# A two-layer graph kernel on one core: weight scaling moved into round 1, a new order of copies from shared PSUM tiles, ACT tables loaded by dummies, decodes issued four blocks ahead

## The chip, the cores and the metric

The kernel runs on one core of one Trainium2 chip. The metric is the device time of one execution in microseconds (us), given as the median of the fast runs; all runs of this study were in the fast state. A ratio is the mean time of one kernel's fast runs over the mean of the other kernel's fast runs of the same rounds, so it is not quite the ratio of the medians quoted beside it. Intervals are 95% intervals.

The engines are called PE (the matmul engine; PEld is its weight load), DVE (VectorE), ACT (ScalarE), POOL (GpSimd) and SP (the queue that issues most transfers).

## The reference, cut to what matters

The reference has N = 3327 nodes with D = 64 features and a dense adjacency of N x N.

```python
# layer 0: attention in hyperbolic space
h = maximum(layernorm(x), 0)
x_t = logmap0(h, c)
left, right = x_t @ w_att[:D, 0], x_t @ w_att[D:, 0]
adj_att = sigmoid(left[:, None] + right[None, :] + b_att) * adj
x_local = logmap(h[:, None, :], h[None, :, :], c)            # N x N x D, never formed by the kernel
x = x + proj(expmap(h, einsum('ij,ijd->id', adj_att, x_local), c), c)
# layer 1: the last <= 100 neighbours of a row, weighted by powers of one half
h = maximum(layernorm(x), 0)
support = h @ weight
mask = adj != 0
rank = cumsum(mask, axis=1);  deg = rank[:, -1:];  k = minimum(deg, 100.0)
pos = rank - (deg - k)
w = mask * where(pos > 0, 0.5 ** (k - pos), 0.0)
x = x + w @ support + bias
```

## The kernel before

The adjacency is worked on in four strips of node columns (8, 8, 6 and 4 blocks of 128). Each strip runs over the 26 row blocks in rounds. In a round, PE forms the pair products `pq`, counts neighbours into `pc` and sums into `po`; ACT takes two Gelu passes over `pq` and makes the sigmoids `sg`; DVE makes the mask and two products, and DVE or ACT reads the counts out as bytes (`behind_lo`, `behind_hi`). Three parts matter here.

**The start.** The node features are turned by PE and copied out of PSUM into `ju` (by DVE) and `jz` (by ACT). A Newton chain and two logarithms then give the factors of the attention logits.

```python
    rsqrt(V, pre, y, v, NB)                       # layer norm
    ...
    def kept(pt, bs, at):
        n = bs.stop - bs.start
        V.tensor_copy(ju[: KB + 7, bs], pt[: KB + 7, at : at + n, :])
        A.copy(jz[:, bs], pt[:, at + n : at + 2 * n, :])
    ...
    p1 = ps.tile([P, 16, P], F16, name="pq", bufs=2)
    turned_to(p1, first_i, 0)                     # PE transposes nu and nz into ONE tile
    p2 = ps.tile([P, 4, P], F16, name="po")
    turned_to(p2, last_j, 0)
    kept(p1, first_i, 0)
    strip_in(0)
    kept(p2, last_j, 0)
    V.tensor_scalar(x2c, x2, MIN_NORM, None, op0=ALU.max)
    rsqrt(V, pre, yr, x2c, NB)                    # three Newton steps, after the copies
    ...
    A.activation(g, g2, AF.Ln, bias=one_c, scale=-0.5)
    ...
    def last_of_ahead():                          # a generator, advanced in rounds 0 and 1
        ...
        yield
        logits((later,))
        left_to_dram()
        yield
        V.tensor_mul(hw[:, :13, :D], rl[:, :13], wide(wn[:, :13], 13))
```

**The change of strip.** At the end of a strip PE transposes its sums into one PSUM tile (`turn`), and two copies bring them to SBUF.

```python
    def per_node(k, pa):
        ...
        for c in range(0, nb, 4):
            ...
            if c == 0:
                A.copy(to, of)
            else:
                V.tensor_copy(to, of)
        return post(agg, k)
```

**The last stage.** ACT and DVE decode 22 of the 26 blocks from bytes in turns to bf16 bit patterns (`wt`, seven buffers; the other four are kept ready, `weight_of` in the traces), and PE multiplies each of the 26 with the features `s` of layer 1. The last strip's nodes are finished meanwhile in small portions (`advance`). Then follow the last blocks, a closing product with the scaled weight `w2s`, and the transfer out.

```python
    w2s = const.tile([P, D], F32, name="w2s")
    V.tensor_scalar(w2s, w2, 2.0**27 / HS, None, op0=ALU.mult)
    ...
        for i, j in enumerate(order):
            if j not in weights:
                weights[j] = decode(j)
            asked_of_act()
            advance(LAST)                         # LAST = 6
            for n in range(len(chunks)):
                add(j, weights[j], n)
            ...
        finish()
        for j in range(late, NB):
            weights[j] = decode(j)
        ...
        for n in range(len(chunks)):
            for j in range(late, NB):
                add(j, weights[j], n)
            ...                                   # copy pw[n] out, then close(n - 2) with w2s
```

## Time and profile before

| Kernel before | us |
|---|---|
| median of the fast runs | 437.38 (437.25 to 437.47, 3 runs) |
| span of the profiled run | 434.5 |
| DVE's first product of adjacency and sigmoid (end of the start) | 42.28 |
| PE's first block of the last stage | 374.57 |
| last closing matmul | 426.83 |

The first view is the page of the kernel before. The first line gives each engine's busy time, its share of the span and its instructions; the row PEclk gives PE's granted clock in tenths in 40 slices of the span.

```profile
PE 364.4 (84%) x1460; PEld 155.8 (36%) x1460; DVE 377.1 (87%) x556; ACT 365.0 (84%) x409; POOL 111.4 (26%) x218
PEclk9999699999999899999999899999996999999987
```

The dips in PEclk (slices 5, 14, 23, 31 and the last two) are worth a look: PE loses clock in the start, at each change of strip and at the end. The trace has no clock record before 40.4 us; PEclk shows full clock there, but PE's 512-column matmuls took 0.63 us at 35.9 us and 0.38 us at 41.3 us. The next view is PE's timeline of the kernel before at the first change of strip (start, duration, engine, line, operation, number of matmuls; in brackets the idle time before and who ended it).

```profile
146.09 1.09 PE L1088 MATMUL po<-ident,sg 65*128 65x65 f32 x8 [1.86 <-ACT sg L1082]
146.97 0.63 PE L629 MATMUL pc<-mask,ca 128*128 128x512 bf16 x1
150.00 3.59 PE L668 MATMUL po<-sg,hw 128*65 128x512 f32 x8
```

PE sits idle for 1.86 us ahead of the transposes, and the matmuls after it take 0.63 us each instead of 0.38: half rate, by the clock records (0.50 from 146.2 to 149.6). So this idle time seems to cost more than itself; the runs below test it. The last view is the table of windows of the kernel before at the third change of strip (stretch, length, busy time and count of PE, PEld, DVE, ACT and POOL, then PE's clock, the transfers' share, GB/s). Its stretches are the steps of 3.41 us at whose edges the trace's clock records change.

```profile
323.68:327.09 3.41, 0.42 (x7) 0.30 (x6) 1.49 (x4) 3.09 (x5) 0.00 (x0) 1.00 0.00 0
327.09:330.50 3.41, 2.21 (x6) 0.83 (x6) 3.38 (x6) 1.01 (x2) 0.86 (x4) 0.50 0.51 154
330.50:333.91 3.41, 3.41 (x6) 0.97 (x5) 2.19 (x3) 2.83 (x4) 2.77 (x8) 0.50 0.20 35
```

After a step in which PE was busy for only 0.42 us, the next runs at clock 0.50. PE is idle for part of that one too (2.21 us busy), and a second at 0.50 follows it, in which PE is full.

### The profile page before, as it was taken

Reading aid. Unit: us, or ns where it says so; the run is one execution under the profiler, and the core shown is the slowest. Engines: PE = TensorE matmul, PEld = TensorE weight load, DVE = VectorE, ACT = ScalarE, POOL = GpSimd, SP = SyncE. Lnnn points to the kernel's source line nnn. Section 1 sums busy time; section 2 is a strip of 40 time slices with the busy share of each in tenths; the row PEclk is TensorE's granted clock in tenths of the full one; section 3 lists DMA queues with packets and bytes.
Section 4 is the critical chain, followed back from the end, with each engine's and each line's share of the span. In section 5 each row is a group of like instructions: output and inputs, shape, how many; then the busy total and the mean of one; then the engine's idle time right before and its main releaser. Section 6 shows DMA issues by size and latency. Waiting matters only on the chain.

```text
span 434.5 us, 4704 instructions
## 1 busy us (share of the span) xinstructions
PE 364.4 (84%) x1460; PEld 155.8 (36%) x1460; DVE 377.1 (87%) x556; ACT 365.0 (84%) x409; POOL 111.4 (26%) x218
## 2 busy tenths in 40 slices
PE   0227499999999899999999899999777999877983
PEld 0014233333333333333333454444332333333453
DVE  2776999999999899999999898899988899688931
ACT  3429599999999989999999899999894999399720
POOL 6010000000000035780160083921505183404200
PEclk9999699999999899999999899999996999999987
DMA  8310444545447435543446354444633320000012
GB/s 186 140 38 0 137 147 144 154 151 172 147 150 206 126 122 159 178 148 99 143 121 181 85 148 141 145 129 138 185 106 99 103 90 0 2 0 1 2 25 62
DMA packets 23248, 48.98 MB, mean 113 GB/s; under 512 B 8713, under 2 KB 9169, under 8 KB 23215
## 3 DMA queue, kind: packets, MB, share of 16 engines
q1 hardware_dynamic: 21087, 47.81, 36.6%
q10 hardware_dynamic: 1808, 0.46, 0.6%
q0 software_dynamic: 320, 0.33, 0.5%
q8 instruction: 13, 0.21, 0.2%
q14 instruction: 20, 0.16, 0.1%
HBM read 46.40 MB, written 0.87 MB: 109 GB/s over the span
## 4 chain that ended last, share of the span: by engine, by line
DVE 38%; ACT 23%; PE 22%; issue 10%; POOL 3%; DMA 2%; POOLq 0%; DVEq 0%; ACTq 0%
DVE sg L1173 11%; DVE sg L1154 10%; PE po L668 8%; ACT sg L651 6%; ACT pq L1147 5%; DVE behind_lo L644 3%; ACT pq L1148 3%; PE pc L629 2%; PE pq L658 2%; PE pq L659 2%; PE pc L630 2%; DVE wt L1207 2%; ACT wt L1205 2%; DVE behind_hi L644 2%; ACT behind_lo L640 2%
## 5 line engine op out<-in xcount | busy, mean ns | idle before, releaser
L668 PE MATMUL po<-sg,hw 128*65 128x512 f32 (+1 forms) x364 | 161.1, 566 | 0.4 <-DVE st L895 0.4
L1173 DVE SCALAR_TENSOR_TENSOR sg<-pq,sg 128x1024 f32<-128x1024 f32 (+1 forms) x91 | 103.8, 1140 | 6.6 <-ACT pq L1148 5.3
L1154 DVE SCALAR_TENSOR_TENSOR sg<-sg,ad 128x1024 f32<-128x1024 f32 (+1 forms) x91 | 103.9, 1142 | 2.5 <-ACT sg L651 2.4
L651 ACT ACTIVATE sg<-left_b,right 128x1024 f32<-128x1024 f32 (+2 forms) x103 | 99.5, 978 | 1.0 <-DVE right L819 1.0
L1147 ACT ACTIVATE pq<-pq 128x1024 f32<-128x1024 f32 (+1 forms) x90 | 86.1, 957 | 4.4 <-PE pq L659 4.3
L1148 ACT ACTIVATE pq<-pq 128x1024 f32<-128x1024 f32 (+1 forms) x90 | 85.2, 946 | 2.9
L630 PE MATMUL pc<-mask,cb 128*128 128x512 bf16 (+1 forms) x182 | 66.9, 378 | 16.3 <-DVE mask L618 14.8
L629 PE MATMUL pc<-mask,ca 128*128 128x512 bf16 (+1 forms) x175 | 65.6, 375 | 13.6 <-DVE behind_hi L644 5.8
L668 PEld LDWEIGHTS po<-sg,hw 128*65 128x65 f32 x364 | 49.5, 138 | 70.1 <-issue 55.1
L658 PE MATMUL pq<-iu,ju 71*128 71x512 f16 (+1 forms) x182 | 68.6, 377 | 1.1 <-ACT jz L755 0.4
L659 PE MATMUL pq<-iz,jz 128*128 128x512 f16 (+1 forms) x182 | 67.0, 375 | 0.0
L618 DVE TENSOR_SCALAR mask<-ad 128x1024 bf16<-128x1024 f32 (+1 forms) x91 | 59.0, 649 | 0.0
L630 PEld LDWEIGHTS <-cb 128*128 128x128 bf16 x182 | 18.1, 99 | 69.7 <-issue 52.0
L1218 PE MATMUL pw<-wt,s 128*128 128x512 bf16 (+1 forms) x154 | 33.9, 371 | 7.4 <-DVE wt L1207 5.1
L967 POOL TENSOR_TENSOR dots<-dots,ih 128x8 f32<-128x8 f32 (+1 forms) x3 | 2.6, 876 | 141.1 <-DVE dots L987 141.1
L629 PEld LDWEIGHTS <-ca 128*128 128x128 bf16 x175 | 17.5, 100 | 30.3 <-issue 18.6
L1218 PEld LDWEIGHTS <-s 128*128 128x128 f16 x182 | 18.0, 100 | 26.8 <-issue 9.3
L658 PEld LDWEIGHTS <-ju 71*128 71x128 f16 x182 | 18.2, 100 | 23.9 <-DVE sg L1173 5.2
L640 ACT ACTIVATE behind_hi<-pc 128x1024 uint8<-128x1024 f32 (+2 forms) x24 | 20.7, 864 | 7.1 <-PE pc L630 7.1
L659 PEld LDWEIGHTS <-jz 128*128 128x128 f16 x182 | 18.4, 101 | 19.9 <-issue 3.5
L640 ACT ACTIVATE behind_lo<-pc 128x1024 uint8<-128x1024 f32 (+2 forms) x29 | 24.9, 858 | 0.0
L1223 POOL TENSOR_TENSOR x_sb<-x_sb,bias_b 128x256 f32<-128x256 f32 (+1 forms) x6 | 9.9, 1660 | 49.6 <-DVE w L1056 44.0
(290 smaller groups left out, 364.8 us busy)
## 6 DMA issues: line engine op xcount, KB each, us to landing
ad<-in_adj_t SPq DMA_DIRECT2D x65, 512.0 KB, 3.6
ad<-in_adj_t SPq DMA_DIRECT2D x26, 384.0 KB, 3.1
out<-o SPq DMA_DIRECT2D x6, 128.0 KB, 2.0
left_b<-left_d SPq DMA_DIRECT2D x1, 512.0 KB, 3.3
x_sb<-in_x ACTq DMA_DIRECT2D x1, 416.0 KB, 5.7
x_sb<-in_x SPq DMA_DIRECT2D x1, 416.0 KB, 4.9
iz<-jz SPq DMA_DIRECT2D x3, 128.0 KB, 2.4
left_b<-left_d SPq DMA_DIRECT2D x1, 384.0 KB
```

The lines of the kernel that those rows point to most:

```text
L618: V.tensor_scalar(*args, 0.0, None, op0=ALU.not_equal)
L629: T.matmul(S.pc[:, f0:f1], ca, S.before[:, f0:f1], start=False, stop=True, skip_group_check=True)
L630: T.matmul(S.pc[:, f0:f1], cb, now[:, f0:f1], start=S.first, stop=True, skip_group_check=True)
L640: A.activation(kept, S.pc[:, : S.F], AF.Relu, scale=128.0 if j in JD else 1.0)
L651: A.activation(part(n, sg, j), S.left[:, : S.F], AF.Tanh, bias=right[:, j : j + 1], scale=0.5)
L658: T.matmul(part(n, pq, j, f0, f1), ju[:KB, j, :], S.iu[:, f0:f1], start=True, stop=False)
L659: T.matmul(part(n, pq, j, f0, f1), jz[:, j, :], S.iz[:, f0:f1], start=False, stop=True)
L668: T.matmul(S.po[: D + 1, f0:f1], hw[:, j, :], part(n, sg_of[n], j, f0, f1), start=j == NB - 1, stop=j == 0)
L1147: A.activation(pq, pq, AF.Gelu, scale=-WG / QS)
L1148: A.activation(pq, pq, AF.Gelu, scale=WH)
L1154: V.scalar_tensor_tensor(sg, sg, 1.0, ad_of.pop(n)[:, :w], op0=ALU.add, op1=ALU.mult)
L1173: V.scalar_tensor_tensor(sg, pq, WD, sg, op0=ALU.add, op1=ALU.mult)
```

## The change

The intent is to take waits off DVE and PE where the engines are not full: in the start, at the changes of strip, and in the last stage. No arithmetic is removed. The core of the diff:

```diff
-PORTIONS, LAST = (2, 4, 4, 8), 6
+PORTIONS, LAST = (2, 4, 4, 8), 8
+LEAD = 4
 ...
     w2 = const.tile([P, D], F32, name="w2")
+    w2s = const.tile([P, D], F32, name="w2s")
 ...                                    # start: two tiles by kind, Newton chain cut in two, tables by dummies
-    p1 = ps.tile([P, 16, P], F16, name="pq", bufs=2)
-    turned_to(p1, first_i, 0)
-    p2 = ps.tile([P, 4, P], F16, name="po")
-    turned_to(p2, last_j, 0)
-    kept(p1, first_i, 0)
+    guess(V, yt, yr, x2c)
+    newton(V, yt, yr, x2c, 1)
+    for src, dst, rows in ((nu, ju, KB + 7), (nz..., jz, P)):
+        pt = ps.tile([P, 16, P], F16, name="pq", bufs=2)
+        ...                             # transposes of src into pt, then copies by DVE (ju) or ACT (jz)
     strip_in(0)
-    kept(p2, last_j, 0)
-    rsqrt(V, pre, yr, x2c, NB)
+    A.activation(load_table, one_c, AF.Ln)
+    newton(V, yt, yr, x2c, 2)
 ...
+    A.activation(load_table, one_c, AF.Gelu)
 ...                                    # last_of_ahead: logits one round earlier
+        logits((later,))
+        left_to_dram()
         wn, opx = small("wn"), small("opx")
 ...
         yield
-        logits((later,))
-        left_to_dram()
-        yield
+        V.tensor_scalar(w2s, w2, 2.0**27 / HS, None, op0=ALU.mult)
 ...
-                    yield LATER if kwargs.get("op") == ALU.pow else 1
+                    yield from [LATER] * 2 if kwargs.get("op") == ALU.pow else [1]
 ...                                    # per_node
             if c == 0:
+                V.tensor_copy(to, of)
+            else:
                 A.copy(to, of)
-            else:
-                V.tensor_copy(to, of)
 ...
-    w2s = const.tile([P, D], F32, name="w2s")
-    V.tensor_scalar(w2s, w2, 2.0**27 / HS, None, op0=ALU.mult)
 ...
+        every = [*order, *range(late, NB)]
 ...
         for i, j in enumerate(order):
-            if j not in weights:
-                weights[j] = decode(j)
+            for jn in every[: i + 1 + LEAD]:
+                if jn not in weights:
+                    weights[jn] = decode(jn)
 ...                                    # the blocks after the loop: decoded there only if not done yet
```

In `kept`, used for later blocks, ACT's copy now also comes ahead of DVE's; `w_h` is computed earlier.

More of the change, by code (lines that the diff above doesn't have):

```diff
@@ L507, in fast, with guess, newton @@
                                 "f_c"))
-    def rsqrt(E, pool, y, v, n):
-        t = pool.tile([P, n], F32, name="rs_t")
+    def guess(E, t, y, v):
         E.tensor_scalar(t.bitcast(I32), v.bitcast(I32), 1, None, op0=ALU.logical_shift_right)
         E.tensor_scalar(y.bitcast(I32), t.bitcast(I32), -1.0, float(0x5F3759DF), op0=ALU.mult, op1=ALU.add)
-        for _ in range(3):
+    def newton(E, t, y, v, steps):
+        for _ in range(steps):
             E.tensor_mul(t, y, y)
@@ L518, in rsqrt @@
             E.scalar_tensor_tensor(y, t, 1.5, y, op0=ALU.add, op1=ALU.mult)
+    def rsqrt(E, pool, y, v, n):
+        t = pool.tile([P, n], F32, name="rs_t")
+        guess(E, t, y, v)
+        newton(E, t, y, v, 3)
     def wide(t, n):
@@ L715, in fast @@
         V.tensor_reduce(rs[:, hs], sr[:, hs], AX.X, ALU.add)
+    w_h = const.tile([P, 2, 2], F16, name="w_h")
+    V.tensor_copy(w_h[:, 0], w_lr)
+    V.tensor_sub(w_h[:, 1], w_lr, w_h[:, 0])
     V.tensor_scalar(v, ss, 1.0 / D, EPS_LN, op0=ALU.mult, op1=ALU.add)
@@ L753, in kept @@
         n = bs.stop - bs.start
+        A.copy(jz[:, bs], pt[:, at + n : at + 2 * n, :])
         V.tensor_copy(ju[: KB + 7, bs], pt[: KB + 7, at : at + n, :])
-        A.copy(jz[:, bs], pt[:, at + n : at + 2 * n, :])
     V.scalar_tensor_tensor(yz, nrm, zs_c, y, op0=ALU.mult, op1=ALU.mult)
@@ L772, in fast @@
     rest(last_j)
-    p1 = ps.tile([P, 16, P], F16, name="pq", bufs=2)
-    turned_to(p1, first_i, 0)
-    p2 = ps.tile([P, 4, P], F16, name="po")
-    turned_to(p2, last_j, 0)
-    kept(p1, first_i, 0)
+    x2c, yr, yt, s, g3 = (small(n) for n in ("x2c", "yr", "yt", "s", "g3"))
+    V.tensor_scalar(x2c, x2, MIN_NORM, None, op0=ALU.max)
+    guess(V, yt, yr, x2c)
+    newton(V, yt, yr, x2c, 1)
+    ends = [*range(first_i.start, first_i.stop), *range(last_j.start, last_j.stop)]
+    for src, dst, rows in ((nu, ju, KB + 7), (nz.rearrange("p b c d -> p b (c d)"), jz, P)):
+        pt = ps.tile([P, 16, P], F16, name="pq", bufs=2)
+        for at, b in enumerate(ends):
+            T.transpose(pt[:rows, at, :], src[:, b, :], id16)
+        for bs, at in ((first_i, 0), (last_j, 8)):
+            copy = A.copy if dst is jz else V.tensor_copy
+            copy(dst[:rows, bs], pt[:rows, at : at + bs.stop - bs.start, :])
     strip_in(0)
-    kept(p2, last_j, 0)
     p3 = ps.tile([P, 16, P], F16, name="pq", bufs=2)
-    x2c, yr, s, g3 = (small(n) for n in ("x2c", "yr", "s", "g3"))
-    V.tensor_scalar(x2c, x2, MIN_NORM, None, op0=ALU.max)
-    rsqrt(V, pre, yr, x2c, NB)
+    load_table = pre.tile([P, 1], F32, name="load_table")
+    A.activation(load_table, one_c, AF.Ln)
+    newton(V, yt, yr, x2c, 2)
     V.tensor_mul(s, x2c, yr)
@@ L797, in fast @@
     A.activation(g3, g3, AF.Square, bias=q0_c, scale=Q1)
+    A.activation(load_table, one_c, AF.Gelu)
     features(later)
     rounded(later)
-    w_h = const.tile([P, 2, 2], F16, name="w_h")
-    V.tensor_copy(w_h[:, 0], w_lr)
-    V.tensor_sub(w_h[:, 1], w_lr, w_h[:, 0])
     V.scalar_tensor_tensor(g3, g3, QK, s, op0=ALU.add, op1=ALU.mult)
@@ L1156, in fast @@
             edges(m + 1)
-        if n == 1:
-            next(rest_of_ahead)
         if two:
@@ L1208, in decode @@
             return wt
-        weights = {j: decode(j) for j in order[: len(JD) + 1]}
+        every = [*order, *range(late, NB)]
+        weights = {j: decode(j) for j in every[: len(JD) + 1]}
         stages.append(Stage(per_node(len(STRIPS) - 1, pa)))
@@ L1237, in fast @@
         for j in range(late, NB):
-            weights[j] = decode(j)
+            if j not in weights:
+                weights[j] = decode(j)
         ow = [l1.tile([P, 512], F32, name="ow", bufs=4)[:, : f1 - f0] for f0, f1 in chunks]
```

## The prediction

> **What bounds the kernel now.** I read the page first: a span of 434.5 us with DVE busy 87%, PE 84% and ACT 84%, so no engine is free and each stage has to be asked by itself. Next I cut the span into stages with a table of windows (first column the stretch, then its length, then busy time and instruction count of PE, PEld, DVE, ACT, POOL).
>
> ```profile
> 0.00:42.00 42.00, 11.88 (x78) 7.34 (x79) 25.38 (x84) 20.49 (x27) 8.49 (x30) 1.00 0.33 94
> 58.00:137.00 79.00, 78.89 (x274) 29.97 (x273) 78.86 (x88) 77.99 (x80) 0.00 (x0) 1.00 0.50 153
> 150.00:234.00 84.00, 82.45 (x281) 30.83 (x280) 82.37 (x89) 81.66 (x87) 35.13 (x62) 1.00 0.46 140
> 373.00:417.00 44.00, 35.83 (x171) 16.52 (x170) 34.34 (x75) 32.02 (x18) 11.60 (x11) 0.99 0.00 1
> ```
>
> In the first two strips PE, DVE and ACT are all full: nothing in the change removes work there, so nothing is to be won inside a strip. The slack is in the start (0 to 42 us), at the three changes of strip, and in the last stage (from 373 us), where the 26 decoded blocks are multiplied. I then read those three in the timelines of single engines (start, duration, engine, line, operation; in brackets how long the engine sat idle first, and who ended it).
>
> ```profile
> 13.01 0.20 DVE L1190 TENSOR_SCALAR w2s<-w 128x64 f32<-128x64 f32 x1 [4.16 <-DMA w<-in_weight]
> 13.12 1.02 DVE L694 SCALAR_TENSOR_TENSOR d<-m,x_sb 128x832 f32<-128x832 f32 x1
> 28.39 0.69 DVE L754 COPY ju<-pq 78x1024 f16<-78x1024 f16 x1 [1.92 <-PE pq L750]
> 42.28 1.23 DVE L1154 SCALAR_TENSOR_TENSOR sg<-sg,ad 128x1024 f32<-128x1024 f32 x1 [2.09 <-ACT sg L651]
> 148.31 0.43 DVE L1100 COPY agg<-po 128x260 f32<-128x260 f32 x1 [1.76 <-ACT agg L1098]
> 325.61 0.29 DVE L1100 COPY agg<-po 128x130 f32<-128x130 f32 x1 [1.92 <-ACT agg L1098]
> ```
> ```profile
> 32.58 1.28 ACT L794 ACT_TABLE_LOAD   x1 [2.17 <-DVE g L792]
> 405.81 8.70 ACT L1205 ACTIVATE wt<-behind_hi 128x3328 uint16<-128x3328 uint8 x3
> ```
> ```profile
> 328.29 0.59 PE L629 MATMUL pc<-mask,ca 128*128 128x512 bf16 x1 [4.19 <-DVE behind_hi L644]
> 414.57 3.22 PE L1218 MATMUL pw<-wt,s 128*128 128x512 bf16 x10 [2.27 <-ACT wt L1205]
> ```
>
> The scaling w2s stands at the end of the source, but the scheduler put it fourth in DVE's queue, where it waits 4.16 us for the last of seven small GpSimd-issued loads, and the second half of the layer norm waits behind it. At the strip changes DVE sits still until ACT, busy with two Gelu passes, has copied its half of the transposed sums. At the end PE's last phase waits for ACT's last three decodes, which ACT could not start before 405.8.
>
> [...] two copies out of one tile run one after the other (the waits of 1.76 and 1.92 us above). So their order is a real choice. [...] a 128x4 pow on POOL took 1.41 us with DVE quiet and 2.62 and 2.59 us when a DVE decode (1.89 us) ran. [...] after the first strip change 512-column matmuls start 0.43 us apart instead of 0.22.
>
> **The change, part by part**, with the order of instructions in both programs (DVE gains three rows, ACT two; PE and POOL keep their counts).
>
> 1. w2s out of the start. The second d (L694) can start at about 8.75 instead of 13.12, which is 4.3 us. Not all of it survives: the next in the queue are masks of the first two adjacency blocks, and the trace's completion signals put those loads at 8.5 and 12.1 us. So the second mask runs from 12.2 and its successor at 12.8, against 15.26: **2.5 us**, less 0.3 for w_h, moved up to before v (its load lands at 12.6, long before). Left: 2.2 us at v.
>
> 2. Transposes in two tiles by kind, half of a Newton chain in front of the copies, tables by dummies. PE transposes from 24.25 (26.46 less 2.2). DVE does six small operations (1.3 us at about 0.22) while it would have waited 1.92 us; ju is copied at 25.55, the rest of the chain ends in g at 28.35 (before: 32.49). ACT copies jz from 26.55 to 27.85, loads Ln's table at once (1.28), takes a dummy (0.2), then Ln and squares (1.12), Gelu's table (1.28), a dummy (0.2), two casts (1.96), and starts Gelu at 34.0 against 38.20. The first sigmoid block waits for PE's transposes of left (36.3 shifted by two casts plus 1.73 and 1.58, so 37.3); DVE's first product starts at about **38.5 against 42.28, 3.8 us**.
>
> 3. Round 0 takes the logits and left_to_dram from round 1. In DVE's queue they now come right after the ju copy, and their matmuls (32 in 1.01 us) need the PSUM tile that this copy frees: DVE waits about 1.1 us, and about 0.3 for the turned left. Before, 0.29 was lost there. The product of round 2, at 54.80 before, comes at about 52.1; the 0.43 us that DVE then waited for PE falls away, since PE and ACT now lead by some 7 us. **Start in all: about 3.0 us.** As DVE is full through the first strip, it hands this on, no more.
>
> 4. Strip changes. DVE copies first, so at 147.2 (end of the PE transposes) instead of 148.31: 1.1 us of DVE, but PE has no gap in the 3 us after and is full after that, so I count 0.3 for the first two changes together. At the third, DVE's copy comes at about 324.2 instead of 325.61, and PE's 4.19 us wait hangs on the DVE work behind it: **1.3 us**.
>
> 5. Last stage. PE needs 26 blocks of 1.39 us, 36 us, and has 44, so its waits decide. I laid DVE's new order out with the old durations: 11 decodes at 1.80 are 19.8 us; what else ran on DVE from 373.53 to its last decode's end at 413.0 is 39.5 less 19.8 less 4.6 idle, 15.1 us; the copy of agg_last adds 0.4. Waits that I expect: 0.55 for transposes, and for POOL 0.2, 0.45, 0.95 and 0.95, in all 3.1. The end is 373.5 + 19.8 + 15.1 + 0.4 + 3.1 = 411.9. ACT now does two decodes instead of three after its last cast and waits: its last ends near 411.0. The last strip's features come later than before (10 decodes ahead of them instead of 8: about 409.9 against 407.6), but still before the last decode. PE's final phase starts at 411.9 instead of 414.57: **2.7 us**. The 20 us after it stay.
>
> Sum: 3.0 + 0.3 + 1.3 + 2.7 = 7.3. 437.4 - 7.3 = **430.1 us**.
>
> **Rivals.** (a) The adjacency loads swallow the start: if the second lands later than 12.1 in an execution, or the logits' wait in round 0 is nearer 2 us, 1.5 us are left of the start: 431.6. For it: 3.4 MB are queued at once; against it: the loads do not depend on the change. (b) The last stage turns on the features: [...] the features land at 412 or later; nothing is won there, 432.8. For it: three waits of 0.9 us on POOL already. Against it: DVE has work in between. (c) DVE's slack at the strip changes does count, because all engines are within 1% of each other, and PE stays at full clock: 2 to 3 us more, 427.5. For it: DVE waited 5.7 us there in sum. Against it: PE has no gap before the features of the third change. (d) The gains are hidden by the full middle: if PE and ACT, not DVE, were what filled strip 1, the start still shifts all of them, so I give this little.
>
> **Range and chances.** (a) and (b) together give 434, (c) with a better end 426.5; the range is 426.5 to 433.5. Faster by over 2% means under 428.6, 1.5 us below my number with an error of some 3 us: 0.30. Slower by 2% would need a new wait of 16 us: 0.01.
>
> **What would show it.** Right: no wait for in_weight on DVE, the second mask near 12.2 with a wait on its load, DVE's first sg product near 38.5, a DVE wait of about 1 us at the logits of round 0, the third strip change's PE wait near 2.9, PE's last phase starting about 7 us earlier than 414.57. Wrong: a first product that is earlier by 3.8 but a first strip that ends no earlier; a PE wait on s instead of wt in the last stage; PE waits that shrink at the first two strip changes.

## The result and the profile after

The changed kernel took **425.63 us** (median of 4 fast runs, 424.87 to 427.22), the kernel before 437.31 us in the same rounds (4 runs, 437.19 to 437.47). The ratio is 0.9737 [0.9709, 0.9766]: faster by more than 2%, and 0.9 us below the range that had been given.

The page of the changed kernel's profiled run (span 423.7 us) has these two lines.

```profile
PE 361.3 (85%) x1437; PEld 155.1 (37%) x1460; DVE 377.9 (89%) x557; ACT 364.6 (86%) x410; POOL 114.0 (27%) x218
PEclk9999989999999999999999899999998999999987
```

The busy times are those of before to within 1% on PE, DVE and ACT: what was removed is idle time. (PE's count is lower because some matmul records are missing from this trace; PEld's is the same.) In PEclk the dip in the start is smaller and one slice later (8 in slice 6 in place of 6 in slice 5), that of slice 31 is smaller (8 in place of 6), and that of slice 14 is gone. DVE's timeline in the changed kernel follows, at the start and at the first and third change of strip.

```profile
8.91 1.03 DVE L702 SCALAR_TENSOR_TENSOR d<-m,x_sb 128x832 f32<-128x832 f32 x1
...
12.06 0.69 DVE L626 TENSOR_SCALAR mask<-ad 128x1024 bf16<-128x1024 f32 x1 [1.52 <-DMA ad<-in_adj_t]
...
38.60 1.23 DVE L1169 SCALAR_TENSOR_TENSOR sg<-sg,ad 128x1024 f32<-128x1024 f32 x1 [1.12 <-ACT sg L659]
...
44.46 0.17 DVE L832 TENSOR_TENSOR left<-po,yr 128x16 f32<-128x16 f32 x1 [1.03 <-PE po L830]
...
144.18 0.43 DVE L1113 COPY agg<-po 128x260 f32<-128x260 f32 x1 [0.28 <-PE po L1103]
...
319.88 0.43 DVE L1113 COPY agg<-po 128x260 f32<-128x260 f32 x1 [0.45 <-PE po L1103]
```

The wait of 4.16 us for the weight is gone; a wait of 1.52 us for the second adjacency block takes part of its place. The first product is 3.68 us earlier than at 42.28. At the changes of strip DVE waits 0.28 and 0.45 us for the transposes, where it had waited 1.76 and 1.92 us for ACT's copy. ACT's timeline in the start of the changed kernel:

```profile
27.82 1.28 ACT L801 ACT_TABLE_LOAD   x1
29.11 0.20 ACT L801 ACTIVATE load_table<-one_c 128x1 f32<-128x1 f32 x1
...
33.63 1.00 ACT L845 ACTIVATE pq<-pq 128x1024 f32<-128x1024 f32 x1
```

The table is loaded at 27.82 (1.28 us; the copy before it ended at 27.80, and ACT's next instruction starts at 29.11) while DVE still works on what the logarithms need, and the first Gelu is at 33.63 instead of 38.20. PE's timeline in the changed kernel, at the first change of strip, at the third, and at the end of the last stage:

```profile
143.44 0.71 PE L1103 MATMUL po<-ident,sg 65*128 65x65 f32 x8 [1.74 <-ACT sg L1097]
...
145.72 3.61 PE L676 MATMUL po<-sg,hw 128*65 128x512 f32 x8
...
322.69 0.38 PE L637 MATMUL pc<-mask,ca 128*128 128x512 bf16 x1 [2.85 <-DVE behind_hi L652]
...
367.89 5.78 PE L1230 MATMUL pw<-weight_of,s 128*128 128x512 bf16 x27
...
402.63 0.60 PE L1230 MATMUL pw<-wt,s 128*128 128x512 bf16 x2 [2.29 <-DVE s L1087]
...
404.43 3.60 PE L1230 MATMUL pw<-wt,s 128*128 128x512 bf16 x9 [0.25 <-DVE wt L1218]
```

Here are the surprises. At the first change PE's idle time is 1.74 us, nearly as before, but PE takes 2.28 us from the transposes to the sums at 145.72, where it had taken 3.91 us (146.09 to 150.00): it did not go to half rate (the clock records have 1.00 from 60.1 to 237.6). At the third change the idle time is 2.85 us instead of 4.19. In the last stage PE's longest wait is now for the features `s`; its final nine matmuls start 36.54 us after its first block (367.89), before 40.00 us.

To compare the sums by part, I use landmarks that both traces have: DVE's product of round 2 (end of the start), the products of rounds 26 and 30 (around the first change), 50 and 62 (second), 76 and 82 (third), and PE's first block of the last stage. The second profile is the same kernel, unedited, in a later run (below).

| Part | predicted gain | changed kernel | same kernel again |
|---|---|---|---|
| start, and the first strip up to round 26 | 3.0 | 2.66 | 2.61 |
| first change (rounds 26 to 30) | 0.3 with the second | 1.60 | -0.02 |
| second change (rounds 50 to 62) | | -0.02 | -0.03 |
| third change (rounds 76 to 82) | 1.3 | 2.41 | 2.43 |
| last stage, from PE's first block to the end | 2.7 | 4.10 | 4.09 |
| **whole span, with the small rest** | **7.3** | **10.79** | **9.12** |

The start is 0.3 to 0.4 us less than predicted; all the surplus lies at the changes of strip and in the last stage.

The figure for the start hangs on which execution it is compared with. Five of the profiled kernels have the start of the kernel before (itself, and the copy order, PE busy, both of these, and the lead, each on it); in them the product of round 26 comes at 139.00, 140.46, 139.94, 139.99 and 139.00 us. In the five profiles with the start of the changed kernel it comes at 136.25 to 136.39. So the table compares with one of the two quickest; against the mean of the five (139.68) the start gains 3.4 us.

### The profile page after: what moved, and what is told of

The parts are those of the page before. It is cut to its first block, busy times and chain, and to the rows that moved or that the text cites. A ratio compares the mean times of both kernels' runs of the same rounds, so it can differ in the third digit from the quotient of the medians.

```text
span 423.7 us, 4689 instructions
## 1 busy us (share of the span) xinstructions
PE 361.3 (85%) x1437; PEld 155.1 (37%) x1460; DVE 377.9 (89%) x557; ACT 364.6 (86%) x410; POOL 114.0 (27%) x218
## 4 chain that ended last, share of the span: by engine, by line
DVE 32%; ACT 28%; PE 21%; issue 12%; POOL 2%; DMA 2%; SPq 0%; POOLq 0%; DVEq 0%; ACTq 0%
ACT sg L659 9%; DVE sg L1186 8%; ACT pq L1162 8%; PE po L676 8%; DVE sg L1169 7%; DVE wt L1218 3%; ACT pq L1163 3%; ACT behind_lo L648 3%; PE pq L666 2%; DMA ad<-in_adj_t 2%; PE pq L667 2%; DVE behind_lo L652 2%; ACT behind_hi L648 2%; PE pc L638 2%; PE pc L637 2%
## 5 line engine op out<-in xcount | busy, mean ns | idle before, releaser
L637 PE MATMUL pc<-mask,ca 128*128 128x512 bf16 (+1 forms) x166 | 60.7, 366 | 15.6 <-DVE behind_hi L652 7.0
L638 PE MATMUL pc<-mask,cb 128*128 128x512 bf16 (+1 forms) x172 | 62.4, 372 | 12.9 <-DVE mask L626 10.6
```

What stands on the lines that cost most here:

```text
L637: T.matmul(S.pc[:, f0:f1], ca, S.before[:, f0:f1], start=False, stop=True, skip_group_check=True)
L638: T.matmul(S.pc[:, f0:f1], cb, now[:, f0:f1], start=S.first, stop=True, skip_group_check=True)
```

## The experiments

The theory that I went in with: the excess is PE's clock. PE falls to half rate for a step of about 3.4 us after a step with little work (in the kernel before at 327.09, after 0.42 us of work in 3.41), and idle time removed at a change of strip or in the last stage removes such steps too. A rival: DVE's time at the changes of strip simply counts in full, and PE's clock follows without costing anything. A second rival for the last stage: the lead of the decodes is worth more than my layout said, whatever the clock does. The twelve kernels ran in three batches, each on another chip, so kernels of different batches are compared only by their ratio to the kernel before (436.44, 436.32 and 435.99 us there). All gave correct outputs.

### The scaling alone

```diff
+    w2s = const.tile([P, D], F32, name="w2s")        # next to w2
 ...
+        V.tensor_scalar(w2s, w2, 2.0**27 / HS, None, op0=ALU.mult)   # last part of last_of_ahead
 ...                                    # its two lines near the end of the source are taken out
```

> Kernel before with w2s moved into round 1 and nothing else. Theory A (the prediction's step 1): DVE's second d starts near 8.9, the second mask waits for its load until 12.1, everything after is 2.5 us earlier, and as all engines move together the time falls by 2.2 to 2.7 us (to about 434.9). Rival B (PE's clock): PE's half-rate windows of 3.4 us fall elsewhere, and one window more or fewer moves the time by a further 1.7 us, so anything from 433 to 436.5, with the span tracking the granted clock.

Measured: 434.37 us (9 runs), ratio 0.9953 [0.9938, 0.9969], 2.07 us by the medians. In the profile the first product came 2.29 us earlier. The step of the prediction that gives 2.2 us at this point holds. What of it reaches the end is less sharp: this profile is 1.68 us ahead at round 26 and 1.30 at round 90, and a further 1.7 us of its span come from the last stage, where this run has no half-rate step. The interval of the ratio is 1.4 to 2.7 us. This is what the expectation's rival B allowed for.

### The copy order alone

```diff
             if c == 0:
-                A.copy(to, of)
+                V.tensor_copy(to, of)
             else:
-                V.tensor_copy(to, of)
+                A.copy(to, of)
```

> Kernel before with DVE copying its half of the transposed sums first at the strip changes, nothing else. Theory S (slack): DVE's waits of 1.76, 2.03 and 1.92 us shrink to about 0.3 to 0.5 us, and about 1.3 us at the first and the third change each reach the end: 2.5 to 3 us. Theory C (clock): PE restarts at half rate after the first change whichever copy is first, so only the third change pays: 1.0 to 1.4 us. The prediction's step 4 said 1.6.

Measured: 433.53 us (6 runs), ratio 0.9939 [0.9919, 0.9960]. The times gain 2.9 us, as theory S said (2.5 to 3), but not where it said: that agreement is luck. The profile's gain at the third change is 2.41 us, at the second -0.10 and at the first -0.05, although DVE did get its copy early there; it loses 1.45 us up to round 26 (the scatter of the start, above) and gains 2.6 us in the last stage, where this run has no half-rate step. DVE's timeline in this kernel at the first change:

```profile
148.28 0.43 DVE L1098 COPY agg<-po 128x260 f32<-128x260 f32 x1 [0.28 <-PE po L1088]
...
156.07 1.22 DVE L644 TENSOR_SCALAR behind_hi<-pc 128x1024 uint8<-128x1024 f32 x1 [2.16 <-PE pc L630]
```

DVE's wait ahead of the copy fell from 1.76 to 0.28 us, and 8 us later DVE stood 2.16 us for PE, whose clock records show half rate from 149.0 to 152.4:

```profile
145.60:149.00 3.40, 1.54 (x14) 0.99 (x14) 3.12 (x6) 3.27 (x5) 0.00 (x0) 1.00 0.53 154
149.00:152.40 3.40, 3.40 (x8) 1.15 (x7) 3.40 (x5) 3.40 (x6) 0.00 (x0) 0.50 0.44 119
```

What DVE had won, it lost to a slower PE. At this change DVE's time seems to count only if PE keeps its clock (here 0.50 in the step from 149.0); the next runs test that.

### PE kept busy at the changes

The product matmuls of the round at the end of a strip are repeated twice into the same PSUM tile, with the same values, so that PE has no gap there.

```diff
         if 0 < n < R - 1:
             products(n + 1)
+            if ended and len(js(n + 1)) == 1:
+                again(n + 1, 2)           # the same matmuls, start=True, into the same pq tile
```

> Kernel before; in the round of each of the first two strip changes PE computes the next product block three times instead of once (same result, written over itself), to fill its gap of 1.86 and 1.94 us before the transposes with work. Theory C (clock): the half-rate windows at 146.2 and 241.8 are gone, PE's next sums start up to 1.7 us earlier, and the time falls by 1 to 3 us. Theory S: DVE is still held until ACT's copy (148.3), so nothing or under 0.5 us.

Measured on the kernel before: 434.81 us (18 runs), ratio 0.9962 [0.9949, 0.9974]. More work made the kernel faster, by 1.6 us by the medians: the profile gains 1.06 us from round 26 to 50 (0.62 of it by round 30), 1.13 at the second change and 0.4 at the third, and the half-rate steps at the first two changes (146.2 and 241.8 in the kernel before) are gone. The transposes of the first change now come with no idle time ahead of them:

```profile
147.02 0.71 PE L1096 MATMUL po<-ident,sg 65*128 65x65 f32 x8
```

> Kernel before with both: DVE copies first, and PE's gap filled. If both are needed at the first change (DVE free at once and PE at full rate), the gain is more than the sum of the two single ones, 4 us or more, with the first change alone giving 1.6 us as in the changed kernel. If the two are independent, the gain is their sum.

Measured with the copy order as well: 431.24 us (5 runs), ratio 0.9879 [0.9860, 0.9899]. The first change gains 1.54 us, the second 1.54 and the third 2.43. From round 26 to 50 the copy order alone gave -0.07, the clock alone 1.06, both 1.54; at the second change they gave -0.10, 1.13 and 1.54: the copy order's 1.5 us of DVE are there to be had, and here they were kept only where PE had no half-rate step. By the times the two parts together (0.0121) are not clearly more than their sum (0.0099); the traces show it, not the times.

### The changed kernel again, unedited

> The changed kernel itself, for its spread on another chip. Theory C (clock): its runs spread over 2 us or more, and the span falls as the granted clock rises, about 1.7 us for each half-rate window of 3.4 us (0.004 of the mean clock). If the spread has another cause, span and clock don't go together. Profile: I expect the windows at the first strip change to be absent or present by chance, as PE's gap there is still 1.7 us.

Measured: 426.84 us (5 runs), ratio 0.9773 [0.9757, 0.9789]. It kept nothing at the first change. The windows of this run around PE's idle time there, cut at the edges of its clock records:

```profile
140.28:143.69 3.41, 1.54 (x10) 0.57 (x8) 3.41 (x5) 3.29 (x5) 0.00 (x0) 1.00 0.47 121
143.69:147.10 3.41, 3.41 (x15) 1.63 (x14) 2.84 (x5) 3.38 (x5) 0.00 (x0) 0.50 0.33 115
```

The first profiled run of the changed kernel around the same idle time, cut in the same way:

```profile
138.64:142.05 3.41, 3.06 (x12) 0.93 (x10) 3.41 (x4) 3.38 (x5) 0.00 (x0) 1.00 0.48 155
142.05:145.46 3.41, 1.97 (x14) 1.23 (x16) 3.13 (x5) 3.38 (x5) 0.00 (x0) 1.00 0.51 154
```

In the first run the idle time was split over two steps, with 3.06 and 1.97 us busy, and the clock stayed at 1.00. In the second it fell wholly into one step, with 1.54 us busy, and the next step was at 0.50. The edges of the steps lie differently against the kernel's start in the two runs: at 138.64 in the first, at 140.28 in the second. So the 1.60 us of the first change in the first profile goes with where the idle time fell on the steps: PE's timeline of the repeated run shows the same program with nearly the same idle time (1.86 us, before 1.74), and half rate after it.

```profile
143.47 1.00 PE L1103 MATMUL po<-ident,sg 65*128 65x65 f32 x8 [1.86 <-ACT sg L1097]
...
147.40 3.59 PE L676 MATMUL po<-sg,hw 128*65 128x512 f32 x8
```

From the transposes to the sums it took 3.93 us here, against 2.28 us in the first profile. Other traces bear this out: of the six with the new copy order and no added work at the changes, the two without a half-rate step at the first change (the changed kernel, and it with the lead taken back) gain 1.60 and 1.62 us there, and the four with one gain between -0.05 and 0.00.

Busy time as these traces count it does not separate the steps that lost full rate from those that kept it. In the kernel before, steps with 1.67 us busy kept it (at 306.6 and 395.4); in the changed kernel one with 1.67 us lost it (at 415.1), and one with 1.70 us kept it (at 39.6). Over the fourteen traces, steps with 1.53 and 1.55 us busy kept it (at 397.3 with PE busy at the changes, at 411.4 with the scaling alone), and in the start 1.91 and 2.17 us lost it (at 41.3 with PE busy everywhere, at 42.9 with the lead taken back).

### PE kept busy in the changed kernel

The same edit as above, on the changed kernel.

> The changed kernel with PE's gaps at the first two strip changes filled by repeating the next product block. Theory C: no half-rate window near 143 and 238; the second change keeps 1.5 us as it did with both edits on the kernel before, so 1.5 to 2 us faster than the changed kernel, and less spread. Rival: the windows there are hidden behind DVE, so no change.

Measured: 423.32 us (5 runs), ratio 0.9717 [0.9694, 0.9741], on the same chip as the repeated run (0.9773). PE's timeline in this kernel at the first change:

```profile
143.35 0.71 PE L1111 MATMUL po<-ident,sg 65*128 65x65 f32 x8
...
145.66 3.65 PE L684 MATMUL po<-sg,hw 128*65 128x512 f32 x8
```

No idle time stands in brackets, and 2.31 us pass to the sums. The half-rate steps of the first two changes are gone (at the first the clock is 1.00 from 139.0 to 149.2), and both changes keep about 1.5 us. The clock is therefore a cause and not a companion: it was changed by added work alone. By the medians this is 3.5 us faster than the repeated run; the profiled run (422.01 us, the fastest of the five) also has no half-rate step in its last stage, worth 1.7 us more (below).

### The lead of the decodes, alone and taken back

```diff
-PORTIONS, LAST = (2, 4, 4, 8), 6
+PORTIONS, LAST = (2, 4, 4, 8), 8
+LEAD = 4
 ...
-                    yield LATER if kwargs.get("op") == ALU.pow else 1
+                    yield from [LATER] * 2 if kwargs.get("op") == ALU.pow else [1]
 ...
-            if j not in weights:
-                weights[j] = decode(j)
+            for jn in every[: i + 1 + LEAD]:
+                if jn not in weights:
+                    weights[jn] = decode(jn)
 ...
```

> Kernel before with the decodes issued four blocks ahead (and eight portions a block, two turns for a power), nothing else. Prediction's step 5: the last phase of PE starts 2.0 to 2.7 us earlier relative to the first block, all of it from fewer decodes after ACT's and DVE's last cast: time down by 2 to 2.7 us. Rival: since the copies of the last strip are not exchanged here, DVE still waits 1.4 us at the reduction[...]: under 1 us.

Measured, on the kernel before: 432.09 us (6 runs), ratio 0.9908 [0.9892, 0.9924]. By the medians this is 4.2 us, more than either theory had said (2 to 2.7, or under 1). The profile gains nothing up to round 90 (-0.07 us) and 4.89 us to the last closing matmul. That is with no half-rate step between PE's first block and the closing matmuls, which the kernel before has at 415.8.

> The changed kernel with the decodes back to one block at a time and six portions. If step 5's cause is right (the lead), it gives back 2 to 3.5 us. If the last stage's gain came from the copy order and from PE's clock in the closing phase, it gives back under 1.5 us.

Measured, the reverse edit on the changed kernel: 429.21 us (5 runs), ratio 0.9838 [0.9824, 0.9852]: 2.8 us of the gain by the ratios are given back against the repeated run on the same chip (0.9773).

The time from PE's first block to the last closing matmul, over eleven profiles, separates lead and clock:

| Lead | Copies swapped | with a half-rate step in it | without |
|---|---|---|---|
| no | no | 52.26, 52.29 (before; with PE kept busy) | 50.60 (scaling alone) |
| no | yes | 51.78, 51.76 (copies and PE busy; lead taken back) | 50.11 (copies alone) |
| yes | no | | 47.31, 47.36 (lead alone; copies taken back) |
| yes | yes | 48.61, 48.59 (changed; again) | 46.91 (PE kept busy) |

Down a column the lead is worth 3.2 to 3.3 us, the copy order 0.4 to 0.5. Along a row the half-rate step costs 1.7 us. Both terms stand in the prediction as one gain of 2.7 us; the changed kernel has them together at 3.7, with the half-rate step as before. So here the second rival holds: the surplus of the last stage is the lead's, not the clock's.

The three other profiles have lead and new copy order too: 48.60 us with a half-rate step (PE busy in the start) and 46.96 without (PE busy everywhere) fit the table; the logits taken back have a step but 47.55 us. That step begins 34.5 us after PE's first block instead of 37.0 us in the changed kernel, and this stage is 0.6 us longer than without a step, not 1.7: a step did not cost the same in both places.

### The copies taken back

The reverse of the copy edit, on the changed kernel.

> The changed kernel with ACT copying first again at the strip changes. From the runs so far: the third change gives back 2.4 us (1.3 of DVE and one half-rate window of PE), the last stage 0.5 us, the first change 0 when PE's window there is at half rate and 1.5 when it is not: 2.9 to 4.4 us slower than the changed kernel. By the prediction's own step 4 it would be 1.6.

Measured: 429.06 us (6 runs), ratio 0.9836 [0.9806, 0.9866]; the changed kernel's two ratios were 0.9737 and 0.9773, on other chips. The third change gives back 2.4 us, and its profile has two half-rate steps there instead of one:

```profile
324.40:327.85 3.45, 2.26 (x6) 0.87 (x6) 3.42 (x6) 1.01 (x2) 0.92 (x4) 0.51 0.52 152
327.85:331.30 3.45, 3.45 (x6) 0.89 (x5) 2.13 (x3) 2.93 (x4) 2.81 (x8) 0.50 0.26 30
```
 The windows of the changed kernel at its third change show what differs when the copy comes early:

```profile
319.50:322.90 3.40, 0.55 (x7) 0.31 (x6) 3.02 (x5) 2.90 (x5) 0.00 (x0) 1.00 0.13 13
322.90:326.35 3.45, 3.45 (x8) 1.24 (x7) 3.42 (x6) 2.09 (x4) 2.13 (x6) 0.51 0.41 144
```

PE is back at 322.69, just ahead of the half-rate step, and fills it; full rate follows at 326.35. In the kernel before it came back inside the step, filled 2.21 of 3.41 us, and got a second one. Over all fourteen profiles the split is clean: the five with the old copy order have two half-rate steps at the third change, the nine with the new one have one. No run has the one without the other, so how the 2.4 us divide into DVE's time and clock is read from the traces and not shown by a run.

The ends of the half-rate stretches sort cleanly by busy time in these traces. Ahead of the end of PE's work, fourteen half-rate steps in which PE was busy for 1.01 to 2.77 us were followed by another, and every one with 2.97 us or more by full rate (2.77 at 326.1 in the scaling alone; 2.97 at 44.6 in the copies taken back).

### The logits taken back

```diff
         kept(p4, low, 0)
-        logits((later,))
-        left_to_dram()
 ...
         yield
+        logits((later,))
+        left_to_dram()
+        yield
 ...                                    # and round 1 advances last_of_ahead again
```

> The changed kernel with the logits of the later blocks and left_to_dram back in round 1. Theory A: the early logits cost DVE 1.0 and 0.2 us of waiting in round 0, so putting them back makes DVE's product of round 2 start 0.3 to 0.8 us earlier and the time up to 0.8 us shorter. Rival: they let ACT and PE run ahead, which is what carries the start's gain into the first strip: putting them back costs 0.5 to 1 us.

Measured: 425.74 us (5 runs), ratio 0.9759 [0.9740, 0.9778]. The product of round 2 comes at 51.46 us, 0.9 us earlier than in the changed kernel, but at round 26 nothing is left of that (2.30 us ahead of the kernel before, against 2.6). Two half-rate steps (46.1 to 52.9) lie in this stretch of this run. This is inconclusive: the move of the logits costs DVE about 1 us in round 0, as predicted, and this study does not show whether it is worth anything later.

### PE busy in the start, and busy everywhere

```diff
+    idle = ps.tile([P, FMAX], F32, name="po")
+    for _ in range(26):                    # ahead of the layer norm's reductions; 8 more ahead of strip_in(0)
+        T.matmul(idle[:, :512], cb, mask_of[1][:, :512], start=True, stop=True)
```

> The changed kernel with 34 matmuls into an unused PSUM tile in PE's idle time of the start (26 after the first counts, 8 after the first transposes), so that PE is at full rate there. Theory C: ten transposes of a kind take 0.55 us instead of 1.05, the copies ju and jz come 0.5 to 1 us earlier, the product of round 0 starts 1 to 2 us earlier; the first strip, bound by DVE, keeps 0.5 to 1.5 us. Rival: the extra matmuls are in the way of the transposes (they end too late): 0 to 2 us slower.

Measured: 425.58 us (6 runs), ratio 0.9738 [0.9711, 0.9766]. In its profile the first product is at 37.75 us (changed kernel 38.60), and at round 26 it is 3.83 us ahead of the kernel before, 1.2 us more than the changed kernel. By the time it can't be told from the changed kernel (0.9737 and 0.9773), and a new half-rate stretch (29.7 to 36.5) came in. A miss: this edit by itself is not shown to be worth anything.

The last kernel joins these, the busy PE at the changes, and ten dummy matmuls into a spare PSUM bank ahead of the final phase.

> The changed kernel with all of PE's gaps filled: the start's 34 matmuls, the repeated product blocks at the first two strip changes, and 10 matmuls into the spare PSUM bank before the closing phase. Theory C: only the window of the third change stays; 1.5 us for the changes as in a_warm, up to 1.5 for the start, up to 1.7 for the end: about 421 to 423 us. Rival: the closing matmuls delay the last phase by as much as they save (no gain over a_warm's 423.3).

Measured: **422.33 us** (5 runs), ratio 0.9684 [0.9665, 0.9703], the lowest ratio of the study, with correct outputs. PE's timeline in this kernel at the end of the last stage:

```profile
397.33 2.32 PE L1272 MATMUL spare<-weight_of,s 128*128 128x512 bf16 x10
399.79 0.60 PE L1246 MATMUL pw<-wt,s 128*128 128x512 bf16 x2
...
401.58 2.10 PE L1246 MATMUL pw<-wt,s 128*128 128x512 bf16 x9 [0.25 <-DVE wt L1233]
```

The dummies take the place of the wait of 2.29 us for `s`. The nine final matmuls take 2.10 us instead of 3.60: the half-rate step ahead of the closing matmuls is gone. That the dummies did this is not shown by one profile: the changed kernel with PE busy at the changes alone has no half-rate step there either in its profile, and its nine take 2.10 us too. By the ratios this kernel (0.9684) can't be told from that one (0.9717, on another chip; the intervals overlap). Against the changed kernel's two ratios it is 0.5 and 0.9% faster.

## Why the prediction was wrong

The prediction said 430.1 us and the result is 425.63. Steps 1 to 3 held; the terms of steps 4 and 5 were too small. In the first profile the surplus of 3.5 us is 1.3 us at the first two changes, 1.1 at the third and 1.4 in the last stage, less 0.3 in the start.

**Steps 1 to 3, the start: right.** The second mask ran at 12.06 after a wait on its load (predicted 12.2), `ju` was copied at 25.44 (25.55), the first Gelu came at 33.63 (34.0), the first product at 38.60 (38.5), and DVE waited 1.03 us at the logits of round 0 (1.1). The sum was 2.66 us at round 26 against 3.0, and 3.4 against the mean of five starts. The scaling alone measured 2.07 us (interval 1.4 to 2.7), so its size is shown that far; the transposes by kind and the dummies were not run alone, and their part (the rest) rests on the timeline. Two readings were off without bearing on the sum: the traces have one more instruction on DVE and one on ACT, not three and two, and the clock of 1.00 in the first window of the prediction is mostly a stretch without clock records.

**Step 4, the first two changes: the size failed, 0.3 us for both.** Its ground was "PE has no gap in the 3 us after and is full after that". What PE does *after* the change was the wrong place to look. PE has a gap of 1.7 to 1.9 us *ahead* of the transposes. In the changed kernel's first profile it lay over two steps of the clock records (3.06 and 1.97 us busy), the clock stayed at 1.00 and 1.60 us were kept; in the second it lay in one step (1.54 us busy), the next was at 0.50 and nothing was kept. With PE kept busy and the new copy order, on either kernel, about 1.5 us are kept at each of the two changes. So the term was short in the first profile and not in the second, by chance: at the ratio of the repeated run, 0.9773, the time here would have been 427.4 us (an estimate from 437.31), inside the range given.

**Step 4, the third change: the size failed, 1.3 us against 2.4.** The part that was worked out is exact: from round 76 to round 80 the changed kernel gains 1.34 us, and PE's wait is 2.85 us (predicted near 2.9). The term left out goes with the second half-rate step, which is missing here, where PE came back at 322.69, ahead of the first one (322.95): another 1.07 us from round 80 to 82.

**Step 5, the last stage: the size failed, 2.7 us against 4.1.** The mechanism held: the final decode and PE's final phase come earlier. PE's last nine matmuls start 36.54 us after its first block, where the layout said 37.3. The layout had 3.1 us of waits on DVE; the trace has 0.56, 0.22, 0.90 and 0.91, in all 2.6, as the expected 0.45 after the first power did not occur: the power was ready at 377.75 and used at 378.10. The waits account for 0.5 of these 0.8 us; the other 0.3 are DVE's busy time, laid out as 35.3 us and measured as 34.9. The remaining 0.6 us lie in "the 20 us after it stay": these took 19.26 us instead of 19.90, of which 0.45 is the landing of the last transfer after the last closing matmul (7.19 instead of 7.64 us). Over all fourteen profiles this landing takes 6.97 to 7.75 us in no order of kernels (7.20 with the copies alone, 7.75 with the lead taken back), so the 0.45 us are scatter and not the change's. The half-rate step in the final phase is in both kernels and is not part of this gain.

**The rivals.** (a) did not come: the load was there at 12.06 us. (b) came in part: PE's wait in the last stage is now on `s`, as named under "wrong", but the wait ended 34.7 us after PE's first block, where the layout had 35.3 (409.9 less 374.57): the features were not late. The two other signs under "wrong" did not come; PE's waits at the first two changes are 1.74 (1.86 in the repeated run) and 1.95 us, before 1.86 and 1.94. (c) was the nearest. It named both DVE's slack and PE's clock and gave 427.5; it was rated low because PE seemed to have no gap. It was wrong in one thing: the two are not added; at the first change the slack counted where the clock stayed at 1.00 (1.60 and 1.62 us) and not where a step at 0.50 followed (-0.05 to 0.00). (d) did not come. The upper end of the range, 433.5, lies under the 434 that the prediction gives for (a) and (b) together.

What is open: no run set where the edges of the clock records' steps fall, so the part they play isn't shown by a run of one program at a chosen phase, only by two runs of one program at two phases (edges at 138.64 and 140.28), by the split of the six traces and by added work. How much of the 1.2 us between the two measurements of the changed kernel (0.9737 and 0.9773, with intervals that overlap) is phase and how much is the chip is not settled.

## What to carry to other kernels

When an idle gap of PE is shortened, ask of the trace's clock records what follows the gap; here a gap of under 2 us (1.86) was followed by half-rate matmuls that took 1.6 us longer (3.91 us from the transposes to the sums, against 2.28), and cheap repeated matmuls in it made the kernel faster (434.81 us, ratio 0.9962). When an engine gets its data earlier at a handover, follow it for the next 10 us: here, with the copy order alone, DVE's wait fell from 1.76 to 0.28 us, 8 us later it stood 2.16 us for PE, and the first change gained -0.05 us. Before a gain in one stage of one profile is believed, run the same kernel once more: 1.6 us here belonged to the run.
